# Products with constants on TensorE before each sampling round's sums, in a four-layer network on one core

## The chip, the cores and the metric

The kernel runs on one core of a Trainium2 chip. Its time is the device time of one execution in microseconds (us), given as the median of several runs. The engines are called as in the profile: PE multiplies matrices, DVE (VectorE) and ACT (ScalarE) do elementwise work, POOL (GpSimd) issues the indirect transfers here, and SP issues the other transfers.

## The reference, cut to what matters

Four images of 256 channels and 64x64 points pass through four layers. Each layer is `x = x + layer(groupnorm(x))`, all in float32. Layer 0 holds the sampling: for every point and each of four groups of 64 channels, nine places are computed from the data, and the image is read there with bilinear weights.

```python
def tap(xi, yi, w):
    valid = (xi >= 0) & (xi < Wi) & (yi >= 0) & (yi < Hi)
    idx = jnp.clip(yi, 0, Hi - 1) * Wi + jnp.clip(xi, 0, Wi - 1)
    v = jnp.take_along_axis(flat, idx.reshape(B, 1, -1), axis=2)
    return v.reshape(B, Cc, *xi.shape[1:]) * (w * valid.astype(img.dtype))[:, None]
...
dout = (samp * mr).sum(-1)                     # nine samples, weighted with a softmax
dout = jnp.einsum('nhwc,oc->nhwo', dout, outproj_w) + outproj_b
x2 = _bn(inp + dout, ...)
x3 = x2 * s                                    # squeeze and excite, s from the mean of x2
m = fc2(leaky_relu(fc1(x3)))
```

Before the sampling, layer 0 has a 1x1 convolution, a 3x3 depthwise convolution, and the 1x1 convolutions that give the places and the weights. Layer 1 is linear attention with a 5x5 depthwise convolution, layer 2 a 3x3 convolution with binarised weights, layer 3 an attention over a pooled image.

## The kernel before

**The sampling.** One image is sampled in 288 rounds (16 blocks of 18; `sample`, L558), four images in 1,152. A round of `gathered` (L592) has POOL issue four indirect transfers (L596), one for each group of channels: each reads, for 128 places, 1 KB from a table in HBM into a tile `g`. There are seven such tiles of four groups, so POOL can be seven rounds ahead of the sums. PE then multiplies what came with the weights `wm`, which ACT makes (L588), and so adds up the samples of each point: eight matmuls of 32 output rows and 128 columns (L603), into a quarter of a PSUM bank called `acc`. The tile has two halves of 256 columns; a half takes two rounds (`UR = 2`), and the halves take turns. After two rounds ACT copies the half to SBUF (`moved`, L608), PE turns it with two transposes (`turned`, L613), and ACT spreads the result (L623). These steps are put off by one, two and three rounds with a table `later`. At the end of a block, PE projects it (`project`, L636) and DVE and ACT finish it.

**What lies beside it.** `run` calls `beside`: after each sampling round it lets other generators go on, in proportion to their costs. Beside image 0 run the convolutions of images 1 to 3 (`convolve`: L373, L394) and their places (`offsets`, L496, with the 3x3 depthwise on DVE). Beside image 1 run the binarising of weights, then the two fully connected layers of image 0 (`feedforward`: L739, L749) and its layer 1 (L821, L870, L943, with the 5x5 depthwise on DVE, L178). Beside images 2 and 3 run the same for the image before, and layers 2 (L1085) and 3 (L1185, L1197, L1203) of the image before that. What is left then runs without sampling.

**The order.** In these stretches the instructions of PE, DVE, ACT and POOL stand on each engine in the order in which the program issues them (`manual_schedule`). SP's transfers are ordered by a scheduler. Each engine takes its instructions in turn, so on PE the sums of a round, the transposes and the matmuls of the other generators stand in one row.

The loop over the rounds, where the change is made:

```python
for i in range(NBLK * BR):
    b, r = divmod(i, BR)
    for f in later.pop(i, ()):
        f()
    if r % UR == 0:
        acc = next(accs)
    gathered(blocks[b], weights[0][0], acc, r)
```

`self.ident` is the 128x128 identity and `self.ow` the output projection's weights (128 partitions, four groups of 256 columns). Both are in SBUF from the start.

Of the kernel before, what the change touches and what calls it, by code (L numbers as in the profile page):

```python
# [17 lines left out]
P = 128  # L18
# [24 lines left out]
STEPS = 900  # L43
CONV, SECOND = NB * 22.5 + 11, 568
# [27 lines left out]
class Net:  # L72
    def __init__(self, ctx, tc, a, out):
        self.tc, self.nc, self.a, self.out, self.kept = tc, tc.nc, a, out, []
        e = ctx.enter_context
        self.cp = e(tc.tile_pool(name="const", bufs=1, side="left"))
        self.ps1 = e(tc.tile_pool(name="ps1", bufs=1, space=PSUM))
        self.mm = e(tc.tile_pool(name="mm", bufs=3, space=PSUM))
        self.banks, self.alone, self.spare = cycle(["mm"]), False, False
        self.dp = e(tc.tile_pool(name="scratch", bufs=1, space=DRAM))  # L80


# [29 lines left out]
    def groupnorm(self, pool, st, name):  # L112

        nc = self.nc
        mv = pool.tile([P, KT, 2], F32, name=name + "_mv")
        for k in range(KT):
            nc.vector.bn_aggr(mv[:, k, :], st[:, k].rearrange("p b s -> p (b s)"))
        yield 2
        pg = self.ps(name + "_pg")
        nc.tensor.matmul(pg[:, 0:KT], self.bd8, mv[:, :, 0], start=True, stop=True)  # L120
        mg = pool.tile([P, KT], F32, name=name + "_mg")
        nc.vector.tensor_copy(mg, pg[:, 0:KT])
        d = pool.tile([P, KT], F32, name=name + "_d")
        nc.vector.tensor_tensor(d, mv[:, :, 0], mg, ALU.subtract)
        nc.vector.tensor_tensor(d, d, d, ALU.mult)
        nc.vector.tensor_tensor(d, d, mv[:, :, 1], ALU.add)
        yield 2
        pv = self.ps(name + "_pv")
        nc.tensor.matmul(pv[:, 0:KT], self.bd8, d, start=True, stop=True)
        sc = self.rsqrt(pool, pv[:, 0:KT], EPS_GN, KT, name)  # L130
        bi = pool.tile([P, KT], F32, name=name + "_bi")
        nc.vector.scalar_tensor_tensor(bi, mg, -1.0, sc, ALU.mult, ALU.mult)
        yield 4
        return sc, bi

    def folded(self, pool, out, w, sc, bi, name):


        nc = self.nc
        n = w.shape[2] // P  # L140
        ps = self.ps(name + "_pb")
        for m in range(n):
            for k in range(KT):
                nc.tensor.matmul(ps[:, m:m + 1], w[:, k, m * P:(m + 1) * P], bi[:, k:k + 1], start=k == 0, stop=k == KT - 1)
        add = pool.tile([P, n], F32, name=name + "_add")
        nc.vector.tensor_copy(add, ps[:, 0:n])
        for k in range(KT):
            nc.scalar.activation(out[:, k], w[:, k], AF.Identity, scale=sc[:, k:k + 1])
        return add
# [104 lines left out]
    def binarise(self):  # L254
# [4 lines left out]
        with self.tc.tile_pool(name="bin", bufs=1, side="left") as sp, \  # L259
# [17 lines left out]
            for i in range(6):  # L277
                nc.tensor.matmul(ps[:, 0:C], self.ones, sums[:, i], start=i == 0, stop=i == 5)
# [27 lines left out]
    def weights(self, pool):  # L306
        nc = self.nc
        w = {}
        for key, name, n in (("cw", "conv_wT", C), ("iw", "inproj_wT", C), ("mw", "offmask_wT", 3 * Q)):
            w[key] = pool.tile([P, KT, n], F32, name=key)  # L310
            nc.sync.dma_start(w[key], self.a[name])

        ps = self.ps()
        for m in range(KT):
            dg = pool.tile([P, P], F32, name=f"dg{m}")
            nc.vector.tensor_scalar(dg, self.ident, self.inv[:, m:m + 1], None, ALU.mult)
            nc.tensor.matmul(ps[:, m * P:(m + 1) * P], self.ones, dg, start=True, stop=True)
        for k in range(KT):
            nc.vector.tensor_tensor(w["cw"][:, k], w["cw"][:, k], ps[:, 0:C], ALU.mult)
        return w  # L320

    def convolve(self, n, w, sp, bp, pads, used):
# [47 lines left out]
        def convolved(b, x, yb, m):  # L370
            ps = self.ps1.tile([P, 512], F32, name="cv", tag="vk")
            for k in range(KT):
                nc.tensor.matmul(ps, cw[:, k, m * P:(m + 1) * P], x[:, k], start=k == 0, stop=k == KT - 1)  # L373
            t = bp.tile([P, 512], F32, name="lk")
            after(1, lambda: nc.scalar.activation(t, ps, AF.Identity, bias=low[:, m:m + 1], scale=SLOPE))
            after(1, lambda: nc.vector.scalar_tensor_tensor(yb[:, m], ps, sh[:, m:m + 1], t, ALU.add, ALU.max))
            after(2, spread, b, yb, m)
# [9 lines left out]
        def projected(b, x, yb, xo, j2):  # L387

            ps = self.ps().rearrange("p (r o) -> p r o", o=C)
            for r in range(2):  # L390
                for h in range(2):
                    at = (4 * h + 2 * j2 + r) * W
                    for k in range(KT):
                        nc.tensor.matmul(ps[64 * h:64 * h + 64, r], yb[:, k, at:at + W], w["iw"][:, k], start=k == 0, stop=k == KT - 1)  # L394
            after(1, added, b, x, yb, xo, j2, ps)
# [80 lines left out]
    def offsets(self, n, c, y, mw, bp, used):  # L476
# [14 lines left out]
        for h in range(2):  # L491
            ps = self.ps().rearrange("p (j o) -> p j o", o=P)
            for j in range(4):
                at = (4 * h + j) * P
                for k in range(KT):
                    nc.tensor.matmul(ps[:, j, 0:3 * Q], t[:, k, at:at + P], mw[:, k], start=k == 0, stop=k == KT - 1)  # L496
            ob = self.row("offmask_b").unsqueeze(1).to_broadcast([P, 4, 3 * Q])
            nc.vector.tensor_tensor(off[:, 4 * h:4 * h + 4], ps[:, :, 0:2 * Q], ob[:, :, 0:2 * Q], ALU.add)
            nc.vector.tensor_tensor(ml[:, 4 * h:4 * h + 4], ps[:, :, 2 * Q:3 * Q], ob[:, :, 2 * Q:3 * Q], ALU.add)
            yield 3  # L500
# [57 lines left out]
    def sample(self, n, ssum):  # L558
# [33 lines left out]
        def gathered(sl, wm, acc, r):  # L592
# [8 lines left out]
            for x in range(2):  # L601
                for i in range(G):
                    nc.tensor.matmul(acc[32 * i:32 * i + 32, :], wm[:, r4, 4 * i + 2 * x:4 * i + 2 * x + 2, :],  # L603
# [29 lines left out]
        def project(b, m):  # L633
            po[m] = self.ps("po")
            for k in range(G):
                nc.tensor.matmul(po[m][:, 0:BR * OB], self.ow[:, k, m * P:(m + 1) * P], dT[b][:, k].rearrange("p r o -> p (r o)"), start=k == 0, stop=k == G - 1)  # L636
# [19 lines left out]
        for i in range(NBLK * BR):  # L656
# [3 lines left out]
            if r % UR == 0:  # L660
                acc = next(accs)
            gathered(blocks[b], weights[0][0], acc, r)
            if r == 0 and b + 1 < NBLK:
# [22 lines left out]
    def feedforward(self, n, ssum, st):  # L686
        nc, tc, a = self.nc, self.tc, self.a
        with tc.tile_pool(name=f"fa{n}", bufs=1, side="right") as sp, \
# [13 lines left out]
            for k in range(KT):  # L702
                nc.tensor.matmul(ps[0:64, 0:1], sd[:, k], mean[:, k:k + 1], start=k == 0, stop=k == KT - 1)
# [4 lines left out]
            for m in range(KT):  # L708
                ps = self.ps()
                nc.tensor.matmul(ps[:, 0:1], su[:, m * P:(m + 1) * P], dn, start=True, stop=True)  # L710
# [21 lines left out]
            for b in range(NB):  # L732
# [3 lines left out]
                for m in range(4 * KT):  # L736
                    ps = self.ps()
                    for k in range(KT):
                        nc.tensor.matmul(ps, f1[:, k, m * P:(m + 1) * P], x2[:, k], start=k == 0, stop=k == KT - 1)  # L739
# [6 lines left out]
                for m in range(KT):  # L746
                    ps = self.ps()
                    for k in range(4 * KT):
                        nc.tensor.matmul(ps, f2[:, k, m * P:(m + 1) * P], hm[:, k], start=k == 0, stop=k == 4 * KT - 1)  # L749
# [7 lines left out]
    def layer1(self, n, st, st2):  # L757
# [3 lines left out]
        with tc.tile_pool(name=f"la{n}", bufs=1, side="right") as sp, \  # L761
# [44 lines left out]
            def rows():  # L806


                for t, tiles in enumerate(((2, 4), (3, 5), (0, 1))):
                    new = lambda c: [self.padded(bp, 1, 20, 2, c, f"pad{i}", bufs=room(3) + (alone and i)) for i in range(2)]  # L810
                    pads = {0: new(0)}
                    for b in range(NB):
# [5 lines left out]
                        for i, m in enumerate(tiles):  # L818
                            ps = self.ps()
                            for k in range(KT):  # L820
                                nc.tensor.matmul(ps, qw[:, k, m * P:(m + 1) * P], x[:, k], start=k == 0, stop=k == KT - 1)  # L821
# [39 lines left out]
            def outer(t, kind, kv, vv, first, last):  # L861
# [15 lines left out]
                def added(i):  # L877
                    for j in range(2):
                        nc.tensor.matmul(sums[:, t, kind], kts[i][:, 1, j], kts[i][:, 0, j],
# [15 lines left out]
            def summed(t):  # L895
# [10 lines left out]
                for kind in range(2):  # L906
                    nc.tensor.matmul(pc[:, kind], ln[:, kind], pw[:, 2 * kind + t], start=True, stop=True)
                    nc.vector.tensor_copy(pw[:, 2 * kind + t], pc[:, kind])

            def output(c, qp, aq):  # L910
# [6 lines left out]
                def dens():  # L917
                    pd.append(self.ps("den"))
                    for h in range(2):
                        for j in range(4):  # L920
                            nc.tensor.matmul(pd[0][32 * j:32 * j + 32], ld[:, j, h], qh[h][j], start=h == 0, stop=h == 1)
# [6 lines left out]
                def head(h, j):  # L928
# [5 lines left out]
                    nc.tensor.matmul(pb[h, j], self.con("sel")[hs, i * P:(i + 1) * P], rd[0][hs], start=True, stop=True)  # L934
# [5 lines left out]
                def proj(h, m):  # L940
                    pr[h, m] = self.ps()
                    for j in range(4):
                        nc.tensor.matmul(pr[h, m], pw[:, j, m * P:(m + 1) * P], ot[h, j], start=j == 0, stop=j == 3)  # L943
# [83 lines left out]
    def layer2(self, n, st, st3, side="left"):  # L1027
# [3 lines left out]
        with tc.tile_pool(name=f"ca{n}", bufs=1, side=side) as sp, \  # L1031
# [45 lines left out]
            for b in range(NB):  # L1077
                v, xv = d, self.block(bp, self.x4_d[n], b, "x4")
                ahead = iter(())
                for m in range(KT):  # L1080
                    for half in range(2):
                        ps = self.long().rearrange("p (e q) -> p e q", e=2)
                        for i in range(12):
                            e, k, t = i // 6, i // 3 % 2, i % 3
                            nc.tensor.matmul(ps[:, e], w[:, k, t, 2 * half + e, m * P:(m + 1) * P], v[:, 2 * half + e, k, t:t + 8],  # L1085
# [14 lines left out]
    def layer3(self, n, st, wide=False):  # L1100
        nc, tc, a = self.nc, self.tc, self.a
        M = HW // 4
        with tc.tile_pool(name=f"na{n}", bufs=1, side="left") as sp, \
# [18 lines left out]
            for k in range(KT):  # L1122
                nc.vector.tensor_scalar(bb[:, k], self.ones, bi[:, k:k + 1], None, ALU.mult)
                nc.tensor.matmul(ps[:, 0:P], bb[:, k], gw[:, k], start=k == 0, stop=k == KT - 1)
# [13 lines left out]
            def first(b):  # L1138
                x = self.block(bp, self.x5_d[n], b, "x5", tag="pT")
                ps = self.ps()  # L1140
                for k in range(KT):
                    nc.tensor.matmul(ps, tw[:, k], x[:, k], start=k == 0, stop=k == KT - 1)
# [11 lines left out]
            def then(b, xq):  # L1154
                ps = self.ps()
                for k in range(KT):
                    nc.tensor.matmul(ps[:, 0:P], fw[:, k], xq[:, k], start=k == 0, stop=k == KT - 1)
                for k in range(KT):
                    nc.tensor.matmul(ps[:, P:2 * P], xq[:, k], gw[:, k], start=k == 0, stop=k == KT - 1)
# [13 lines left out]
            for b in range(NB):  # L1173
                m2 = bp.tile([P, 512], F32, name="m2")
                for j in range(4):
# [8 lines left out]
                    for i in range(2):  # L1184
                        nc.tensor.matmul(s[i], tv[:, 4 * b + j], ph[:, i * 512:(i + 1) * 512], start=True, stop=True)  # L1185
# [16 lines left out]
                    for m in range(8):  # L1202
                        nc.tensor.matmul(ps[:, 0:P + 1], pT[:, m], gt[:, m], start=m == 0, stop=m == 7)  # L1203
# [7 lines left out]
                for k in range(KT):  # L1211
                    ps = self.ps()
                    nc.tensor.matmul(ps, ww[:, k * P:(k + 1) * P], m2, start=True, stop=True)
# [170 lines left out]
```

## Time and profile before

| What | Value |
|---|---|
| median of 3 runs | 7,716.53 us (7,714.51 to 7,720.85) |
| the profiled execution | 8,695.07 us |
| its span | 8,693.3 us |
| instructions in it | 99,761 |
| mean granted clock of PE | 0.803 |
| busy: PE, weight loads, DVE, ACT, POOL | 5,880, 3,499, 4,818, 3,541, 4,935 us |
| gathers (L596) | 4,608 |
| matmuls of the sums (L603) | 18,432 in the trace |

The page gives each engine's busy time, the span in 40 slices (a digit is a tenth of the slice, and for PEclk a tenth of full clock), and groups of instructions. A row of a group has its line, engine, operation, `out<-in`, shapes and count, then busy time and mean nanoseconds of one, and then the idle time of the engine just before such instructions with what ended most of it ("<-"). "issue" is time in which the engine waited for nothing that the profile shows; "remote" is a release whose origin it does not show. The start of a matmul is measured and its end is modelled. The profiled execution is 979 us longer than the median, so times within it are set against its own span.

### The profile page before, as it was taken

Reading aid. Unit: us, or ns where it says so; the run is one execution under the profiler, and the core shown is the slowest. Engines: PE = TensorE matmul, PEld = TensorE weight load, DVE = VectorE, ACT = ScalarE, POOL = GpSimd, SP = SyncE. Lnnn points to the kernel's source line nnn. Section 1 sums busy time; section 2 is a strip of 40 time slices with the busy share of each in tenths; the row PEclk is TensorE's granted clock in tenths of the full one; section 3 lists DMA queues with packets and bytes.
Section 4 is the critical chain, followed back from the end, with each engine's and each line's share of the span. In section 5 each row is a group of like instructions: output and inputs, shape, how many; then the busy total and the mean of one; then the engine's idle time right before and its main releaser. Section 6 shows DMA issues by size and latency. Waiting matters only on the chain.

```text
span 8693.3 us, 99761 instructions
## 1 busy us (share of the span) xinstructions
PE 5880.0 (68%) x35776; PEld 3498.6 (40%) x35776; DVE 4817.7 (55%) x6045; ACT 3541.0 (41%) x10767; POOL 4934.7 (57%) x4870
## 2 busy tenths in 40 slices
PE   4454554448744446688876676888766778986899
PEld 2232222224323222234644443345544333664476
DVE  5344442443366667324776675228766762699833
ACT  2333333234444433334445443444454442456414
POOL 2666666466666666666666556666655560476410
PEclk7676766669866667799988887999878879998899
DMA  6454554444533334444543344445433342220131
GB/s 172 129 160 123 145 149 118 114 143 148 158 107 106 110 109 126 137 127 138 142 133 111 111 116 138 146 135 142 141 105 111 112 118 96 74 72 29 44 97 54
DMA packets 744383, 1031.75 MB, mean 119 GB/s; under 512 B 354128, under 2 KB 459984, under 8 KB 742352
## 3 DMA queue, kind: packets, MB, share of 16 engines
q0 software_dynamic: 221184, 604.27, 24.4%
q1 hardware_dynamic: 522704, 421.10, 16.4%
q8 instruction: 283, 4.64, 0.2%
q14 instruction: 212, 1.74, 0.1%
HBM read 856.39 MB, written 168.61 MB: 118 GB/s over the span
## 4 chain that ended last, share of the span: by engine, by line
PE 43%; another core or an unknown queue 17%; DVE 17%; ACT 13%; issue 8%; DMA 1%; POOL 0%; SPq 0%; ACTq 0%; DVEq 0%; POOLq 0%
DVE agg L178 10%; PE acc L603 6%; PE ps L739 5%; PE ps L749 5%; ACT wm L588 5%; PE ps L1085 4%; PE ps L821 3%; PE ps L943 2%; PE ps L1203 2%; PE s L1185 2%; PE po L636 2%; ACT dT L623 2%; ACT at L608 1%; PE rden L934 1%
## 5 line engine op out<-in xcount | busy, mean ns | idle before, releaser
L596 POOL DMA_INDIRECT g<-tab,sl x4608 | 4399.0, 955 | 2790.8 <-issue 1179.7
L178 DVE SCALAR_TENSOR_TENSOR agg<-pad,vec,agg 128x1024 f32<-128x1024 f32 x2280 | 2934.5, 1287 | 63.9
L603 PE MATMUL acc<-g,wm 128*32 128x128 f32 x18432 | 1012.4, 336 | 2022.6 <-ACT at L608 1471.8
L603 PEld LDWEIGHTS acc<-g,wm 128*32 128x32 f32 x18432 | 557.7, 129 | 2524.7 <-ACT at L608 1683.4
L588 ACT ACTIVATE wm<-sl,con 128x48 f32<-128x48 f32 x6144 | 1490.1, 366 | 26.0 <-remote 12.6
L1085 PE MATMUL ps<-xd,w 128*128 128x256 f32 x3072 | 741.0, 392 | 37.6 <-issue 30.1
L623 ACT COPY dT<-dp 64x128 f32<-64x128 f32 x1152 | 297.2, 258 | 985.8 <-remote 524.3
L1085 PEld LDWEIGHTS ps<-xd,w 128*128 128x128 f32 x3072 | 587.3, 196 | 159.0 <-issue 79.0
L739 PE MATMUL ps<-x2f,f 128*128 128x512 f32 x1024 | 502.3, 639 | 10.2 <-issue 5.1
L608 ACT COPY at<-acc 128x256 f32<-128x256 f32 x576 | 214.5, 372 | 712.8 <-remote 607.4
L821 PE MATMUL ps<-xr,qw 128*128 128x512 f32 x768 | 463.5, 733 | 21.8 <-issue 8.5
L724 DVE SCALAR_TENSOR_TENSOR hm<-ps,vec,lk 128x512 f32<-128x512 f32 x256 | 190.6, 750 | 502.4 <-ACT lk L741 375.2
L749 PE MATMUL ps<-hm,f 128*128 128x512 f32 x1024 | 463.6, 601 | 0.0
L741 ACT ACTIVATE lk<-ps,low 128x512 f32<-128x512 f32 x256 | 174.0, 687 | 514.7 <-PE ps L739 413.2
L636 PE MATMUL po<-dT,ow 128*128 128x288 f32 x1024 | 336.7, 477 | 56.5 <-issue 13.8
L875 ACT COPY kt<-pt 128x512 f32<-128x512 f32 x256 | 149.5, 585 | 544.8 <-remote 246.8
L1036 POOL TENSOR_TENSOR xd<-xp 128x640 f32<-128x640 f32 x64 | 79.8, 1275 | 497.3 <-DMA xq<-x 280.3
L1203 PE MATMUL ps<-gt,pT 128*128 128x129 f32 x2048 | 316.5, 315 | 47.1 <-ACT pT L1199 32.9
L613 PE MATMUL dp<-ident,at 128*128 128x128 f32 x1152 | 285.5, 336 | 77.1 <-ACT dT L623 53.4
L1203 PEld LDWEIGHTS ps<-gt,pT 128*128 128x128 f32 x2048 | 297.2, 226 | 98.8 <-ACT pT L1199 45.0
L1185 PE MATMUL s<-ph,th 128*128 128x512 f32 x512 | 289.2, 677 | 42.9 <-DVE ot L938 9.2
L739 PEld LDWEIGHTS ps<-x2f,f 128*128 128x128 f32 x1024 | 199.2, 203 | 253.3 <-issue 238.5
(243 smaller groups left out, 7710.6 us busy)
## 6 DMA issues: line engine op xcount, KB each, us to landing
g<-tab,sl POOLq DMA_INDIRECT x4608
x<-x SPq DMA_DIRECT2D x128, 512.0 KB
xr<-x SPq DMA_DIRECT2D x96, 512.0 KB
tab<-xo SPq DMA_DIRECT2D x192, 128.0 KB
x<-in_x SPq DMA_DIRECT2D x32, 512.0 KB
y<-yc SPq DMA_DIRECT2D x32, 512.0 KB
yb<-y SPq DMA_DIRECT2D x64, 256.0 KB
x<-yb SPq DMA_DIRECT2D x64, 256.0 KB
```

What stands on the lines that cost most here:

```text
L178: nc.vector.scalar_tensor_tensor(to, s, wt, acc, ALU.mult, ALU.add)
L588: nc.scalar.activation(wm[:, :, :, o], blocks[b][:, r:r + WR, G:], AF.Copy, scale=self.con("own")[:, o:o + 1])
L596: nc.gpsimd.indirect_dma_start(out=g[:, i, :], out_offset=None, in_=table, in_offset=bass.IndirectOffsetOnAxis(ap=sl.bitcast(I32)[:, r, i: ...
L603: nc.tensor.matmul(acc[32 * i:32 * i + 32, :], wm[:, r4, 4 * i + 2 * x:4 * i + 2 * x + 2, :], g[:, i, x * P:(x + 1) * P], start=x == 0, st ...
L623: nc.scalar.copy(dT[b][hs, :, r:r + UR], dp[u][hs, :, :, s, :].rearrange("p v g o -> p g v o"))
L636: nc.tensor.matmul(po[m][:, 0:BR * OB], self.ow[:, k, m * P:(m + 1) * P], dT[b][:, k].rearrange("p r o -> p (r o)"), start=k == 0, stop=k ...
L739: nc.tensor.matmul(ps, f1[:, k, m * P:(m + 1) * P], x2[:, k], start=k == 0, stop=k == KT - 1)
L749: nc.tensor.matmul(ps, f2[:, k, m * P:(m + 1) * P], hm[:, k], start=k == 0, stop=k == 4 * KT - 1)
L821: nc.tensor.matmul(ps, qw[:, k, m * P:(m + 1) * P], x[:, k], start=k == 0, stop=k == KT - 1)
L1085: nc.tensor.matmul(ps[:, e], w[:, k, t, 2 * half + e, m * P:(m + 1) * P], v[:, 2 * half + e, k, t:t + 8], start=i % 6 == 0, stop=i % 6 == 5)
L1185: nc.tensor.matmul(s[i], tv[:, 4 * b + j], ph[:, i * 512:(i + 1) * 512], start=True, stop=True)
L1203: nc.tensor.matmul(ps[:, 0:P + 1], pT[:, m], gt[:, m], start=m == 0, stop=m == 7)
```

## The change

A counter `work` adds up what each matmul in the program writes: twice the columns of its output, scaled by the output's partitions over 128. Transposes are not counted. Before the sums of a round, PE is given products of `ident` with columns of `ow` until the counter has reached 2,048; after the round's sums have been issued, the counter is set to zero. So a round's products depend on how much matmul work the other generators issued since the round before. The products are written to the part of `acc` that the coming sums overwrite: in an even round the whole half (256 columns, 512 of work each, at most four), in an odd round its second quarter (128 columns, 256 of work each, at most eight). Nobody reads them.

```diff
+ALIVE = 2048
...
-        self.banks, self.alone, self.spare = cycle(["mm"]), False, False
+        self.banks, self.alone, self.spare, self.work = cycle(["mm"]), False, False, 0
...
+    def of(self, out):
+
+        self.work += 2 * out.size() // P
+        return out
...
-                nc.tensor.matmul(ps, cw[:, k, m * P:(m + 1) * P], x[:, k], start=k == 0, stop=k == KT - 1)
+                nc.tensor.matmul(self.of(ps), cw[:, k, m * P:(m + 1) * P], x[:, k], start=k == 0, stop=k == KT - 1)
...
             if r % UR == 0:
                 acc = next(accs)
+            while self.work < ALIVE:
+                free = acc[:, r % UR * P:]
+                nc.tensor.matmul(self.of(free), self.ident, self.ow[:, 0, 0:free.shape[1]], start=True, stop=True)
             gathered(blocks[b], weights[0][0], acc, r)
+            self.work = 0
```

The wrapping with `self.of(...)` is the same at every other matmul of the program and changes none of them.

## The prediction

> **What bounds the kernel now.** I read the page's slices first, then the busy time by stage, the rows and waits of the gathers and their sums, and one stretch in order of time.
>
> ```profile
> POOL 2666666466666666666666556666655560476410
> PEclk7676766669866667799988887999878879998899
> L596 POOL DMA_INDIRECT g<-tab,sl x4608 | 4399.0, 955 | 2790.8 <-issue 1179.7
> L603 PE MATMUL acc<-g,wm 128*32 128x128 f32 x18432 | 1012.4, 336 | 2022.6 <-ACT at L608 1471.8
> ```
>
> Gathers fill the slices up to about 7,200 us, with POOL at 6 tenths whatever the other engines do. PE's clock is low in the first half. The sums (L603) issue for 1,012 us and stand idle for twice that, mostly until ACT's copy of the bank (L608).
>
> Busy time by sampling stage (images 0 to 3, then the rest without sampling); the columns are the stretch, its length, PE, weight loads, DVE, ACT and POOL with counts, clock, DMA share and GB/s:
>
> ```profile
> 137.00:1908.00 1771.00, 813.50 (x6476) 462.97 (x6476) 701.95 (x999) 597.50 (x2225) 1107.02 (x1152) 0.65 0.48 136
> 1908.00:3615.00 1707.00, 1018.38 (x6708) 533.92 (x6708) 979.22 (x1033) 681.63 (x2373) 1100.59 (x1153) 0.74 0.43 125
> 3615.00:5405.00 1790.00, 1332.42 (x8482) 795.13 (x8480) 1061.93 (x1281) 795.65 (x2575) 1096.56 (x1153) 0.86 0.45 129
> 5405.00:7210.00 1805.00, 1353.55 (x8583) 806.62 (x8585) 1064.50 (x1285) 798.10 (x2583) 1094.82 (x1152) 0.86 0.44 125
> 7210.00:8693.00 1483.00, 1282.86 (x5174) 859.88 (x5163) 914.03 (x1279) 638.24 (x958) 535.04 (x256) 0.92 0.21 66
> ```
>
> All four sampling stages take 1,707 to 1,805 us although PE's busy time differs by two thirds and its clock by a third. So neither sets the pace alone: what they share is 1,152 gathers. In order of time a gather starts every 1.255 us when nothing holds it (0.95 us and 0.30 us of issue), so 4,608 need 5,783 us. They take 7,054 us (137 to 7,191): POOL stands for 1,271 us, **18%**.
>
> What it stands for, in the waits of POOL:
>
> ```profile
> POOL g L596 <- issue: 1179.7, 3860, 0.6
> POOL g L596 <- PE acc L603: 648.2, 252, 36.7
> POOL g L596 <- remote: 578.1, 292, 3.5
> ```
>
> The first row is the 0.30 us between gathers. The others are waits for a buffer: there are 7, and PE's sums free them. "Remote" has no releaser in the records; it is 2 us at a time, at the start of a round. I take it for the same wait. And why PE is late, in order of time (image 1):
>
> ```profile
> 2996.21 0.37 ACT L608 COPY at<-acc 128x256 f32<-128x256 f32 x1
> 2996.63 1.08 PE L603 MATMUL acc<-g,wm 128*32 128x128 f32 x16 [1.41 <-ACT at L608]
> 2997.65 0.69 PE L613 MATMUL dp<-ident,at 128*128 128x128 f32 x2
> 2998.26 1.08 PE L603 MATMUL acc<-g,wm 128*32 128x128 f32 x16
> 3004.97 0.53 ACT L623 COPY dT<-dp 64x128 f32<-64x128 f32 x2 [5.54 <-remote]
> 3005.16 0.94 POOL L596 DMA_INDIRECT g<-tab,sl  x1 [1.94 <-remote]
> 3005.84 0.37 ACT L608 COPY at<-acc 128x256 f32<-128x256 f32 x1 [0.34 <-remote]
> 3006.27 1.08 PE L603 MATMUL acc<-g,wm 128*32 128x128 f32 x16 [6.93 <-ACT at L608]
> ```
>
> PE does two rounds, ACT copies them out, PE does the next two: a **loop PE, ACT, PE** of one turn in two rounds. In the built program the sums of every pair wait for the copy of the pair just before, although the two pairs use different halves of the bank. POOL is up to 7 rounds ahead, held by this loop.
>
> The profiled execution took 8,695.1 us (span 8,693.3 and 1.8 outside); the median without a profile is 7,716.5, 979 us less. The rest after 7,210 us is full of PE work, so I let nearly all of that fall on the sampling: 7,054 - 979 = 6,075 us, only 292 us above POOL's 5,783. In the timed runs POOL then stands for at most **5%**.
>
> **The Trainium skill.** "TensorE: Matmul & The Clock Gate", Part 1, says that PE runs at half clock until a window of some 3.4 us was busy, and returns to it after an idle one. The trace agrees on the window and is stricter on the rest: the clock changes in steps of 3.41 us; a slow window busy for 95% or more is followed by a full one in 9 of 10 cases, one busy for under 80% never; a full window busy for under 35% is never followed by another, so PE need not be idle to lose it. The sums take 1.08 us a round slow and 0.65 at full clock. I go by the trace: 1.75 us of products in a round of 5 don't keep the clock by themselves. "PSUM — Partial Sum Buffer", on bank collisions, has accesses of two engines to one bank and quadrant kept apart by semaphores, whichever columns they touch; the wait for ACT's copy of the other half, 1,472 us above, is such a one. The new products write to the same bank and so inherit it.
>
> **The change, part by part.** (1) *What is added.* In the built program 450 of 1,152 rounds get products: 176, 152, 61 and 61 of the four images; 209 of them are even rounds with 720 products of 256 columns, 241 odd ones with 1,612 of 128. Together 390,656 columns: 167,936, 128,000, 47,360 and 47,360. Each is issued to the chip in two passes, as every matmul but the transposes is (18,432 rows of L603 for 9,216 in the code). Price of a pass in a dense warm stretch:
>
> ```profile
> 8306.88 11.82 PE L1085 MATMUL ps<-xd,w 128*128 128x256 f32 x54
> ```
>
> 11.82 / 54 = 0.219 us for 256 columns with its weight load, 0.855 ns a column, so 1.71 ns a column of product: warm 287, 219, 81 and 81 us, twice that at half clock. A round without other work gets 1,024 columns, 1.75 us warm, 3.5 us cold.
>
> (2) *What clock that gives.* Busy time times clock is the work at full clock: now 529, 754, 1,146, 1,164 us, or 30%, 44%, 64%, 64% of the stages at clocks 0.65, 0.74, 0.86, 0.86. With the products it is 816, 973, 1,227, 1,245 us, or 46%, 57%, 69%, 69%; along those pairs the clock becomes about 0.75, 0.82, 0.88, 0.88 (an estimate from the rows above). The products then cost 383 + 267 + 92 + 92 = 834 us of PE's time. The work already there gets shorter: 813 (1 - 0.65/0.75) = 108, 1,018 (1 - 0.74/0.82) = 99, 1,332 (1 - 0.86/0.88) = 30, and 31: 268 us. Net PE is **566 us** longer busy: the saved time doesn't pay for the products.
>
> (3) *Where it stands.* In the built program an even round's first product carries the wait for ACT's copy, the products follow, then the sums. So they don't fill PE's idle time ahead of that wait; they start when it ends and push back the sums, the two transposes behind them, ACT's next copy, and every matmul of the other streams queued on PE. That is inside the loop. In odd rounds they stand between two things that were ready.
>
> (4) *What hides it.* POOL needs 5.02 us a round, and the products go to rounds with little other work: with 1.75 us of products, 0.65 of sums and 0.2 of a transpose, a warm round is half of that. Where PE isn't what POOL waits for, they cost nothing. I take as the share paid the share of time for which POOL stands: 5% (28 us) is the lower end, the profiled 18% (102 us) the upper; products in rounds that would have been used to catch up can bring 30% (170 us). I take **10%: 57 us**, as the loop gets longer where it had slack. 7,716.5 + 57 = 7,773. In a profiled execution I expect the 18%: about 8,797.
>
> (5) *What moves.* DVE and POOL keep their order. On ACT 12 scalings of weights (0.37 us each) stand behind some copies once. On SP some 65 of 1,559 transfers stand elsewhere, all among neighbours; the largest step is one block's index loads behind about 15 stores and table rows (0.3 to 0.7 us each to issue). They are wanted a block later, some 90 us, so I cost them at nothing; without that cover the longest wait of that line in SP's queue, 27.6 us, is the price. The count itself is made while building and costs nothing.
>
> **The rivals.** *Slower, fully paid.* If PE's loop and not POOL sets the pace in the timed runs too, most of the 566 us is paid: 60% is 340 us, 8,056. For it: POOL nearly always waits for PE in the profile. Against it: 979 us vanish without the profile.
> *Nothing.* If POOL's 1.255 us is the pace and products always lie beside it: 7,716. For it: equal stages at clocks of 0.65 to 0.86.
> *Faster.* The rounds that hold POOL are heavy ones, without products: they gain from a PE still warm from the round before (sums 1.08 to 0.65, transposes 0.69 to 0.44) and pay nothing. Images 0 and 1 have 591 of POOL's 1,271 us, so 136 of the 292; half of it back gives 7,648. In PE's total the point is a clock of 0.96 to 1.0 in images 0 and 1 (816/813, 973/1,018); it decides below that only if the light rounds are all hidden. For it: in image 0 POOL stands 0.32 us a gather while the clock is low and 0.22 while it is full. Against it: in image 1 that is 0.24 and 0.21, and in images 2 and 3, mostly at full clock, 0.30.
>
> **The numbers.** About 0.2%, 15 us, is what a measurement of this kernel tells from no change. Partly paid, 7,745 to 7,886, likeliest 7,773: 0.51. Fully paid, 8,056: 0.06. Nothing: 0.17. Faster, 7,648: 0.26. Range 7,640 to 7,900; left out are the fully paid case and the farther part of the faster one.
>
> **What would show it.** Right: sums' row unchanged in count, 4,664 new passes; clock near 0.75 in image 0; PE some 550 us busier before 7,210; even products released by ACT's copy; POOL's waits for PE longer. Wrong: POOL standing less than 1,271 us, or clocks above 0.9 in images 0 and 1 with the sums at 0.65 us throughout.

## The result and the profile after

The changed kernel takes 7,803.9 us (median of 4 runs, 7,799.6 to 7,809.0), the kernel before in the same comparison 7,716.8: a ratio of 1.0113 [1.0095, 1.013], **87 us more**.

One thing has to be known to read what follows. The kernel before takes 8,756 us on one of the three chips on which the experiments ran, and 7,721 and 7,723 on the other two (each chip was used for one set of runs). Its profile at the top of this document (8,695 us) lies near the one chip, and all its timed runs, and those of the changed kernel, agree with the other two; which chip that profile came from is not on record. So the profile after is set against another profile of the unchanged kernel, taken on one of the quick chips (the first experiment; span 7,723.4 us).

The page of the changed kernel: POOL and clock in 40 slices, then the gathers (L602, before L596), the sums (L609, before L603) and the products (L670).

```profile
POOL 2777777776777777767666567676666531966220
PEclk8999898899999988999898889999888899988899
L602 POOL DMA_INDIRECT g<-tab,sl x4608 | 4406.9, 956 | 1915.1 <-issue 1262.7
L609 PE MATMUL acc<-g,wm 128*32 128x128 f32 x18432 | 1005.0, 296 | 785.4 <-ACT at L614 455.7
L670 PE MATMUL acc<-ow,ident 128*128 128x128 f32 (+1 forms) x4664 | 923.1, 355 | 250.8 <-ACT at L614 250.6
```

The clock is 8 or 9 tenths from the first slice on. The sums take 1,005 us of PE; in the quick profile of the unchanged kernel they take 1,294. The products wait 250.6 us for ACT's copy (L614), a wait that was the sums'. PE is busy for 6,247.5 us against 5,933.0.

Busy time by stage in the unchanged kernel (quick chip; images 0 to 3, then the rest). The first number after the stretch is its length, the next PE's busy time; the last three are PE's clock, the DMA share and GB/s:

```profile
137.00:1603.00 1466.00, 961.34 (x6599) 500.87 (x6600) 715.37 (x1025) 606.68 (x2263) 1107.22 (x1153) 0.70 0.57 164
1603.00:3071.00 1468.00, 1097.99 (x6667) 550.05 (x6667) 967.19 (x1009) 674.18 (x2342) 1099.40 (x1152) 0.78 0.49 145
3071.00:4654.00 1583.00, 1253.25 (x8480) 760.69 (x8479) 1059.23 (x1281) 792.21 (x2575) 1097.65 (x1152) 0.89 0.50 146
4654.00:6238.00 1584.00, 1257.40 (x8489) 762.99 (x8482) 1059.96 (x1282) 792.27 (x2575) 1098.20 (x1152) 0.89 0.49 143
6238.00:7723.00 1485.00, 1284.01 (x5184) 861.55 (x5184) 913.02 (x1279) 637.95 (x958) 534.42 (x256) 0.92 0.21 66
```

And in the changed kernel:

```profile
138.00:1608.00 1470.00, 1078.78 (x8568) 719.40 (x8568) 715.14 (x1025) 606.85 (x2263) 1111.85 (x1152) 0.89 0.57 164
1608.00:3079.00 1471.00, 1154.79 (x8189) 692.17 (x8186) 967.49 (x1009) 675.03 (x2342) 1098.46 (x1153) 0.93 0.49 145
3079.00:4702.00 1623.00, 1324.31 (x9067) 841.10 (x9066) 1059.57 (x1281) 793.03 (x2575) 1098.18 (x1152) 0.91 0.49 142
4702.00:6324.00 1622.00, 1324.93 (x9073) 840.73 (x9072) 1060.40 (x1282) 793.04 (x2575) 1098.37 (x1152) 0.91 0.48 139
6324.00:7807.00 1483.00, 1283.88 (x5183) 860.98 (x5181) 912.85 (x1279) 638.18 (x958) 534.54 (x256) 0.92 0.21 66
```

Images 0 and 1 got 76% of the columns and are 4 and 3 us longer. Images 2 and 3 got 24% and are 40 and 38 us longer. The rest is unchanged. The clock rose in images 0 and 1 by 0.19 and 0.15, and that bought no time.

The waits of POOL, and of PE, show why (total us, times, longest; images 0 and 1, then images 2 and 3). In the unchanged kernel (quick chip):

```profile
POOL g L596 <- PE acc L603: 33.2, 32, 7.7
PE acc L603 <- DMA g<-tab,sl: 481.6, 606, 13.9
...
POOL g L596 <- PE acc L603: 316.5, 162, 6.6
PE acc L603 <- ACT at L608: 423.7, 178, 8.4
```

In the changed one:

```profile
POOL g L602 <- PE acc L609: 37.3, 38, 4.5
PE acc L609 <- DMA g<-tab,sl: 316.8, 392, 13.2
...
POOL g L602 <- PE acc L609: 397.2, 183, 6.6
PE acc L609 <- ACT at L614: 296.5, 129, 8.3
```

In images 0 and 1 PE waits for gathered data: it is early, and the products fill time in which it would have waited. Its waits for ACT's copy stay as they were there (321 us, then 311 with those of the products) and cost nothing. In images 2 and 3 PE waits for gathered data for 3 us in all in the unchanged kernel; POOL waits for PE, and for 81 us longer with the products.

One place, in the same rounds of image 2, shows the mechanism. Columns of a timeline: start, length, engine, instruction, and in brackets the idle time before and its releaser. Unchanged kernel (quick chip):

```profile
3883.38 0.20 ACT L631 COPY dT<-both 128x16 f32<-128x16 f32 x1 [5.46 <-DVE both L630]
...
3884.02 1.08 PE L603 MATMUL acc<-g,wm 128*32 128x128 f32 x16 [7.82 <-ACT at L608]
...
3894.97 0.37 ACT L608 COPY at<-acc 128x256 f32<-128x256 f32 x1
3895.39 1.06 PE L603 MATMUL acc<-g,wm 128*32 128x128 f32 x16 [3.50 <-ACT at L608]
3896.74 0.95 POOL L596 DMA_INDIRECT g<-tab,sl  x1 [0.44 <-PE acc L603]
...
4014.13 0.69 PE L613 MATMUL dp<-ident,at 128*128 128x128 f32 x2 [0.45 <-ACT dT L623]
4014.75 1.08 PE L603 MATMUL acc<-g,wm 128*32 128x128 f32 x16
4016.13 0.94 POOL L596 DMA_INDIRECT g<-tab,sl  x1 [0.94 <-PE acc L603]
```

Changed kernel:

```profile
3910.95 0.37 ACT L614 COPY at<-acc 128x256 f32<-128x256 f32 x1
3911.38 3.78 PE L670 MATMUL acc<-ow,ident 128*128 128x256 f32 x8 [3.50 <-ACT at L614]
3915.09 1.08 PE L609 MATMUL acc<-g,wm 128*32 128x128 f32 x16
3916.47 0.94 POOL L602 DMA_INDIRECT g<-tab,sl  x1 [4.19 <-PE acc L609]
...
4037.55 0.69 PE L619 MATMUL dp<-ident,at 128*128 128x128 f32 x2 [0.91 <-ACT dT L629]
4038.03 3.62 PE L670 MATMUL acc<-ow,ident 128*128 128x128 f32 x16
4041.58 1.08 PE L609 MATMUL acc<-g,wm 128*32 128x128 f32 x16
4042.97 0.94 POOL L602 DMA_INDIRECT g<-tab,sl  x1 [4.35 <-PE acc L609]
```

In the even round PE had waited 3.50 us for ACT in both kernels. After that wait the clock is low, so the products take 3.78 us for eight passes (0.47 each), not 1.75. The sums come 3.7 us later after the copy than before, and the gather that waits for their buffer stands 4.19 us in place of 0.44: POOL pays all of it. In the odd round it is the same, 4.35 for 0.94. These rounds are light on PE by the program's count, but POOL is at the end of its buffers there. Some 11 us before the even round, PE had stood 7.82 us for ACT's copy, which came behind an ACT instruction that had waited 5.46 us for DVE (L631, at the end of a block; in the changed kernel 7.95 and 5.58 us). So PE can be behind by waiting as well as by work, and a count of a round's work does not tell whether it has time to spare.

### The profile page after: what moved, and what is told of

The parts are those of the page before. It is cut to its first block, busy times and chain, and to the rows that moved or that the text cites. A ratio compares the mean times of both kernels' runs of the same rounds, so it can differ in the third digit from the quotient of the medians.

```text
span 7807.3 us, 108885 instructions
## 1 busy us (share of the span) xinstructions
PE 6247.5 (80%) x40440; PEld 3994.9 (51%) x40440; DVE 4811.5 (62%) x6045; ACT 3535.5 (45%) x10767; POOL 4942.1 (63%) x4870
## 4 chain that ended last, share of the span: by engine, by line
PE 40%; DVE 18%; POOL 7%; ACT 6%; issue 6%; DMA 3%; SPq 0%; DVEq 0%; POOLq 0%; ACTq 0%
DVE agg L184 12%; POOL g L602 6%; PE ps L749 6%; PE ps L759 6%; PE acc L609 4%; PE ps L1095 4%; PE acc L670 3%; PE ps L831 3%; PE ps L1213 2%; PE s L1195 2%; PE ps L953 2%; PE po L642 2%; DMA g<-tab,sl 1%; DVE mx L1196 1%; PE pt L1207 1%
## 5 line engine op out<-in xcount | busy, mean ns | idle before, releaser
L602 POOL DMA_INDIRECT g<-tab,sl x4608 | 4406.9, 956 | 1915.1 <-issue 1262.7
L609 PE MATMUL acc<-g,wm 128*32 128x128 f32 x18432 | 1005.0, 296 | 785.4 <-ACT at L614 455.7
L609 PEld LDWEIGHTS acc<-g,wm 128*32 128x32 f32 x18432 | 533.7, 114 | 1313.1 <-ACT at L614 592.3
L670 PE MATMUL acc<-ow,ident 128*128 128x128 f32 (+1 forms) x4664 | 923.1, 355 | 250.8 <-ACT at L614 250.6
L670 PEld LDWEIGHTS acc<-ow,ident 128*128 128x128 f32 x4664 | 759.9, 224 | 359.9 <-ACT at L614 312.6
L1095 PE MATMUL ps<-xd,w 128*128 128x256 f32 x3072 | 716.1, 385 | 6.0 <-DVE x L1079 3.5
L749 PE MATMUL ps<-x2f,f 128*128 128x512 f32 x1024 | 473.0, 609 | 1.8 <-ACT f L724 1.8
L614 ACT COPY at<-acc 128x256 f32<-128x256 f32 x576 | 214.5, 372 | 476.6 <-PE acc L609 442.8
L831 PE MATMUL ps<-xr,qw 128*128 128x512 f32 x768 | 403.9, 652 | 12.5 <-ACT pT L1209 5.6
L642 PE MATMUL po<-dT,ow 128*128 128x288 f32 x1024 | 294.4, 434 | 29.9 <-ACT dT L637 14.2
L1213 PEld LDWEIGHTS ps<-gt,pT 128*128 128x128 f32 x2048 | 274.9, 211 | 70.7 <-ACT pT L1209 31.9
L1213 PE MATMUL ps<-gt,pT 128*128 128x129 f32 x2048 | 290.9, 299 | 23.4 <-ACT pT L1209 19.5
L759 PEld LDWEIGHTS ps<-hm,f 128*128 128x128 f32 x1024 | 189.2, 190 | 225.9 <-issue 224.8
```

The source lines that it names most:

```text
L602: nc.gpsimd.indirect_dma_start(out=g[:, i, :], out_offset=None, in_=table, in_offset=bass.IndirectOffsetOnAxis(ap=sl.bitcast(I32)[:, r, i: ...
L609: nc.tensor.matmul(self.of(acc[32 * i:32 * i + 32, :]), wm[:, r4, 4 * i + 2 * x:4 * i + 2 * x + 2, :], g[:, i, x * P:(x + 1) * P], start=x ...
L642: nc.tensor.matmul(self.of(po[m][:, 0:BR * OB]), self.ow[:, k, m * P:(m + 1) * P], dT[b][:, k].rearrange("p r o -> p (r o)"), start=k == 0 ...
L670: nc.tensor.matmul(self.of(free), self.ident, self.ow[:, 0, 0:free.shape[1]], start=True, stop=True)
L749: nc.tensor.matmul(self.of(ps), f1[:, k, m * P:(m + 1) * P], x2[:, k], start=k == 0, stop=k == KT - 1)
L759: nc.tensor.matmul(self.of(ps), f2[:, k, m * P:(m + 1) * P], hm[:, k], start=k == 0, stop=k == 4 * KT - 1)
```

## The experiments

In what follows, **standing** is the sum over consecutive gathers of the time between their starts above 1.251 us, and **net PE** the increase of PE's busy time in a stage, products added less what the rest got shorter. Both are worked out from the traces.

**1. The unchanged kernel again.** No edit.

> The kernel before, unchanged, for a second profile. In the first one the waits of an origin that the records don't show took 17% of the chain, and the profiled execution was 979 us over the median; in the changed kernel's profile there are none, and it agrees with its median within 5 us. If the 979 us belong to the kernel before whenever it is profiled, this execution takes about 8,690 us again, with about 1,270 us of POOL standing. If they belonged to that one execution, it takes about 7,720 us, and POOL stands for some 290 us, nearly all of it in images 2 and 3.

Measured: 7,725.1 us with the profile on (span 7,723.4, clock 0.837), and no "remote" wait at all. So the 979 us between the first profile and the median do not come from the profiling as such. That they belong to a chip is read from experiments 5 to 8, where 13 runs of the kernel before take 8,734 to 8,774 us. As the prediction assumed, nearly all of the difference lies in the sampling: it lasts 6,099 us here and 7,054 there. Standing is 25, 29, 143 and 144 us in the four images.

**2. Products beside images 0 and 1 only** (295,936 of 390,656 columns).

```diff
-            while self.work < ALIVE:
+            while n < 2 and self.work < ALIVE:
```

> Products only beside images 0 and 1: 328 rounds, 295,936 of the 390,656 columns. In the changed kernel's profile POOL stands for 29 us in each of images 0 and 1 and 181 us in each of 2 and 3. Theory A (POOL's own pace hides the products beside images 0 and 1, and images 2 and 3 pay for theirs): within 0.2% of the kernel before, 7,700 to 7,732 us. Theory B (every product is paid at the same small share, as predicted): 76% of the columns, so 76% of 87 us, about 7,783 us. Theory C (a warmer PE helps there): below 7,700 us.

Measured: 7,723.6 us, ratio 1.0002 [0.9993, 1.001], at a clock of 0.903. Three quarters of the products, and whatever they move in the order of ACT and SP, neither cost nor gain anything.

**3. Products beside images 2 and 3 only** (94,720 columns).

```diff
-            while self.work < ALIVE:
+            while n > 1 and self.work < ALIVE:
```

> Products only beside images 2 and 3: 122 rounds, 94,720 columns. Theory A: the whole loss, about 7,804 us (87 us for 162 us of products at full clock). Theory B: 24% of it, about 7,738 us. A third theory, that the other order of SP's transfers costs the 87 us and not the products, has no fixed number for either kernel.

Measured: 7,801.3 us, ratio 1.0102 [1.0086, 1.0117], 79 us more. One quarter of the products is nearly the whole loss.

**4. Half of the set amount.**

```diff
-ALIVE = 2048
+ALIVE = 1024
```

> The bound is 1,024 instead of 2,048 in all images. Theory A: the loss goes with the columns that are left in images 2 and 3; with a bound of half, at most half the columns are left in each round that has any, so a loss of 20 to 45 us, 7,737 to 7,762 us. Theory B: half of the columns or less, 7,745 to 7,760 us. If it is the number of rounds with a product, or the added wait for ACT's copy, and not the time of the products: nearly the whole loss, about 7,790 us.

Measured: 7,750.4 us, ratio 1.0036 [1.0022, 1.0049], 28 us more. In images 2 and 3 there are 33,792 columns now, and 28 / 33,792 is 0.83 ns a column; in experiment 3 it is 79 / 94,720 = 0.83. That is half of the 1.71 ns that a column takes on PE.

**5 to 8, on the chip where the kernel before takes 8,756 us.** The first two exchange halves of the two PSUM tiles `acc` and `dp`, so that the sums of consecutive pairs of rounds go to two different tiles, and no longer wait for ACT's copy of the pair just before. First without products (5), then with (6):

```diff
-        def halves(name):
-
-            t = self.ps1.tile([P, 2, 256], F32, name=name, tag=name)
-            return cycle([t[:, 0], t[:, 1]])
-
-        accs, dps = halves("acc"), halves("dp")
+        banks = [self.ps1.tile([P, 2, 256], F32, name=name, tag=name) for name in ("acc", "dp")]
+        accs, dps = cycle([banks[0][:, 0], banks[1][:, 0]]), cycle([banks[1][:, 1], banks[0][:, 1]])
```

> The kernel before with the halves of two PSUM banks exchanged: bank one holds the sums of even pairs and the transposes of odd ones, bank two the others. The sums of a pair then no longer wait for ACT's copy of the pair just before; only the transposes wait for a copy, one round later. Theory A1 (the loop PE, ACT, PE of one turn in two rounds is what holds PE beside images 2 and 3, and so holds POOL): POOL stands clearly less than the 287 us of images 2 and 3, and the time falls by 40 to 150 us, to between 7,570 and 7,680 us. Theory A2 (PE's own work in heavy rounds holds it, the wait for the copy is slack): 7,700 to 7,735 us.

> The changed kernel with the banks exchanged in the same way: products as before, but none of them waits for ACT's copy of the pair just before. A1: the products fall into time in which PE stood, so the time is close to that of the exchanged kernel without products, within 30 us. A2: 80 us or more above it, as PE's time is what is paid.

Measured: 8,660.7 us without products, ratio to the kernel before 0.9888 [0.987, 0.9907], 96 us less, which by its size fits theory A1; 8,733.0 with them, 0.9968 [0.9954, 0.9982]. The products cost 72 us, which lies between the two readings of experiment 6 and nearer to A2. In the profile without products POOL stands 274 to 332 us in every image, with 749 us of its waits called "remote", and the products add 20 to 24 us of standing in each of the four images, the first two included. So what is hidden depends on the chip too. The changed kernel without the exchange was not run on this chip.

The next two leave the halves as they were. Experiment 7 has the products of experiment 3, but of 16 columns each; experiment 8 has the full ones up to twice the set amount (`n > 1` and `ALIVE = 4096`, 356,352 columns).

```diff
-            while self.work < ALIVE:
+            while n > 1 and self.work < ALIVE:
                 free = acc[:, r % UR * P:]
-                nc.tensor.matmul(self.of(free), self.ident, self.ow[:, 0, 0:free.shape[1]], start=True, stop=True)
+                nc.tensor.matmul(self.of(free)[:, 0:16], self.ident, self.ow[:, 0, 0:16], start=True, stop=True)
```

> Products only beside images 2 and 3, the same number (590), each written with 16 columns in place of 128 or 256, and counted as before. If the columns are the cost: 94,720 columns become 9,440, and the loss falls from 79 to about 10 us, 7,730 us. If the added instructions and waits are the cost, it stays near 7,800 us.

> Products only beside images 2 and 3, with a bound of 4,096 in place of 2,048: 328 rounds and 356,352 columns, 609 us of PE at full clock. With half the bound the loss was 28 us for 33,792 columns there, with the bound of 2,048 it was 79 us for 94,720: 0.83 ns a column both times, half of a column's 1.71 ns. Theory A: more rounds are now filled to 3.5 us of products, with sums, transposes and other work above POOL's 5.0 us, so the share paid rises from a half towards all: loss 350 to 600 us, 8,070 to 8,320 us. If the share stays at a half: about 8,020 us.

Measured: narrow 8,841.4, ratio 1.0095 [1.008, 1.0111], 85 us more; double 8,948.0, 1.0223 [1.0205, 1.0242], 192 us more. Experiment 7 fits its second reading: a tenth of the columns costs no less, so the price does not go with columns. Experiment 8 missed both of its readings (some 300 us, or 350 to 600): 3.8 times the columns brought the clock of the two images to 0.93. What the price goes with could not be read on this chip alone, for lack of the full products beside them. Hence the last four.

**9 to 12, on a chip where the kernel before takes 7,720.9 us:** the kernels of 5, 6, 7 and 3 once more.

> The kernel before with the halves of the two banks exchanged, so that the sums of a pair of rounds don't wait for ACT's copy of the pair just before. Theory (the loop of PE, ACT and PE holds POOL in images 2 and 3): on a chip where the kernel before takes about 7,720 us, POOL's standing of 143 and 144 us in images 2 and 3 falls by half or more, 7,580 to 7,690 us; on a chip where it takes about 8,756 us, again some 1.1% less. Rival (PE's own busy time or the gathers' transfers hold POOL there): within 15 us of the kernel before where that takes 7,720.

> The changed kernel with the same exchange of halves. Theory (products cost time because they lengthen the loop): on a chip where the kernel before takes 7,720 us, at most 30 us over the kernel of the exchange alone, against 87 us without it. Rival (the products cost PE's time in order, loop or not): 70 to 95 us over the exchange alone, as the 72 us seen where the kernel before takes 8,756.

Measured: without products **7,528.4 us, ratio 0.9749 [0.9735, 0.9762]**, 193 us less than the kernel before and the fastest version here; with products 7,565.7, 0.9798 [0.9784, 0.9811]. The products cost 37 us, where they cost 87 without the exchange. That is over the 30 that the theory gave, and far under the 70 to 95 of its rival.

Images 2 and 3 by busy time without products (the columns as above):

```profile
3062.00:4557.00 1495.00, 1244.95 (x8481) 751.92 (x8480) 1057.02 (x1281) 786.95 (x2575) 1101.28 (x1152) 0.90 0.52 154
4557.00:6056.00 1499.00, 1247.28 (x8483) 754.65 (x8482) 1057.75 (x1282) 787.46 (x2575) 1103.98 (x1152) 0.90 0.51 151
```

And the waits of POOL for the sums of the two tiles in the whole execution:

```profile
POOL g L592 <- PE acc L599: 64.3, 41, 8.3
POOL g L592 <- PE dp L599: 51.1, 50, 6.1
```

PE has as much to do as before, at 0.90 of its clock for 0.89, and yet the stages are 88 and 85 us shorter. POOL's waits for the sums fall from 349.6 us to 115.4, its standing in images 2 and 3 from 287 to 112. So in these two images it is mostly the loop of PE, ACT and PE that holds POOL, with whatever makes ACT's copy late, and not PE's work alone.

> Products in images 2 and 3 only, the same 590 in the same rounds, but each of 16 columns: 9,440 columns for 94,720. If the loss goes with the columns (PE's time): 5 to 20 us over the kernel before, of the 79 us that the full ones cost. If it goes with the number of products or with the wait for ACT's copy that the first one carries: 60 to 85 us, as the 85 us seen on the chip where the kernel before takes 8,756.

> The full products in images 2 and 3 only, beside the narrow ones on one chip. Where the kernel before takes 7,720 us: 79 us over it as seen before, so 7,795 to 7,810. Where it takes 8,756: if columns count, 60 us or more over the narrow ones, near 8,900; if the number of products or the wait counts, within 25 us of the narrow ones, near 8,850.

Measured: full 7,797.0, ratio 1.0098 [1.0083, 1.0114], 76 us more; narrow **7,865.7, 1.019 [1.0177, 1.0204], 145 us more**. Both readings of experiment 11 missed: a tenth of the columns costs nearly twice as much. Images 2 and 3 with the full products:

```profile
3072.00:4691.00 1619.00, 1326.48 (x9054) 841.44 (x9052) 1059.71 (x1281) 791.93 (x2574) 1096.68 (x1152) 0.91 0.48 143
4691.00:6313.00 1622.00, 1325.35 (x9074) 840.95 (x9078) 1060.38 (x1282) 792.83 (x2577) 1097.17 (x1152) 0.91 0.48 139
```

With the narrow ones, and one even round's products in order of time:

```profile
3067.00:4705.00 1638.00, 1345.97 (x8997) 868.03 (x8998) 1057.74 (x1279) 791.35 (x2570) 1097.73 (x1153) 0.88 0.48 141
4705.00:6354.00 1649.00, 1360.74 (x9071) 875.41 (x9072) 1059.25 (x1281) 793.67 (x2576) 1097.52 (x1152) 0.87 0.47 137
...
3905.73 1.78 PEld L670 LDWEIGHTS acc<-ow,ident 128*128 128x128 f32 x8 [3.74 <-ACT at L614]
3905.74 1.89 PE L670 MATMUL acc<-ow,ident 128*128 128x16 f32 x8 [3.50 <-ACT at L614]
```

Eight passes of 16 columns take 1.89 us at low clock, and the loads of 128 columns of weights beside them 1.78, so 0.22 each: as much as a pass of 128 columns in the odd round above (3.62 / 16 = 0.23), half of one of 256. The load sets the price of a narrow pass. The Trainium skill ("TensorE: Matmul & The Clock Gate", "LDWEIGHTS (loading the stationary operand)") has the load's time go with the columns of the weights and not with their rows. The changed kernel's trace agrees on the rows: the shortest load of 64 rows by 128 columns takes 0.182 us, of 128 by 128 0.186, of 128 by 32 0.106, though a quarter of the columns is not a quarter of the time. So the narrow products still take 101 us of PE an image, the full ones 125. And they leave the clock at 0.88 and 0.87, under the 0.89 without products, where the full ones bring 0.91: the rest of PE's work gets 51 and 57 us shorter with the full products (1,253 - (1,326 - 125), and so on) but only 8 in image 2, and none in image 3, with the narrow ones. Why narrow passes do less for the clock was not tried by itself.

Standing and net PE of images 2 and 3 together, each against its own reference (1 for the upper four rows, though 11 and 12 ran on the other quick chip; 9 for the last). The share is the added standing by the net PE time:

| Kernel | net PE, us | more standing, us | share | loss in images 0 and 1: net PE, standing |
|---|---|---|---|---|
| changed kernel | 139 | 78 | 0.56 | 174, 7 |
| half (4) | 63 | 32 | 0.51 | 80, 1 |
| full, images 2 and 3 (12) | 141 | 74 | 0.52 | none added |
| narrow (11) | 196 | 120 | 0.61 | none added |
| exchange with products (10) | 114 | 33 | 0.29 | 170, -5 |

One rule covers the rows without the exchange: in images 2 and 3, 0.5 to 0.6 of the net PE time is paid, in images 0 and 1 next to nothing. With the exchange it is 0.29. Set against the first profile, which is not of the same set of runs, experiment 7 gives 197 and 116 us (0.59) and experiment 8 456 and 210 us (0.46). Of the 133 us by which the narrow kernel's profiled execution is longer, some 16 lie behind the sampling; I did not follow them.

## Why the prediction was right, and where it was not

The direction, the mechanism and roughly the size held: "partly paid", 7,773 us forecast for 7,804 measured. But two terms of the sum were off in opposite ways: the net PE time was 1.8 times too large, the share paid 2.8 times too small. That their product came out near is luck. Of the signs named, the passes, the release by ACT's copy and POOL's longer waits for PE came; a clock near 0.75 and a PE some 550 us busier did not. POOL standing less than 1,271 us, named as a sign of being wrong, came too (425 us), but that sum belonged to the first profile: against the quick one it rose from 341.

**(1) What is added.** Right: 4,664 passes in the trace. They take 923 us of PE against 834 forecast.

**(2) The clock.** Mis-sized. Along the rows of the first profile the forecast was 0.75, 0.82, 0.88 and 0.88; measured are 0.89, 0.93, 0.91 and 0.91. So much more of PE's time is saved: 610 us (923 - 313), the sums alone 289, against 268 forecast. Net PE is 313 us longer busy (117, 57, 71 and 68 by image), not 566. In experiment 6 products did bring 0.79, 0.84, 0.88 and 0.88, near the forecast (0.66, 0.73, 0.86 and 0.87 without, in experiment 5): the rows were read rightly, but the timed runs are not like them. The clocks alone do not give the 610 us. With the clocks of the two quick profiles, the forecast's own formula gives 205 + 177 + 28 + 28 = 438 us, an estimate. Its premise, that busy time times clock is the work, does not hold: image 0 without products is 529 us by it in the first profile and 961 * 0.70 = 673 in the quick one (its sums 299 and 497 us busy). With the products these sums fell to 336 us, to 0.68, where the clocks' ratio is 0.79. That fits sums which are issued piece by piece as their data comes, and less so with products ahead of them: PE stood for gathered data 606 times in images 0 and 1, and 392 times then. The clock rule also left a gap between 35% and 80%. In the changed kernel's trace, of the full windows busy for 50 to 65% only 14% (of 204) are followed by a slow one, of those busy for 35 to 50% it is 84% (of 90); a warm round with products, 1.75 + 0.65 + 0.2 of 5.02 us, is busy for some 52%.

**(3) Where it stands.** Right, and seen in the timeline: the even products took over the wait for ACT's copy and pushed back the sums. The loop carries more than half of the price on a quick chip: 87 us became 37 once the sums no longer waited for the copy just before. In the odd round shown the products did the same harm without a wait of their own.

**(4) What hides it.** This is the step that failed: one share, 10%, for all products. Measured over all it is 87 / 313 = 28%, but the mean says little: it is 0.04 in images 0 and 1 (7 of 174 us) and 0.56 in images 2 and 3. POOL's standing in the timed runs was judged well, 292 us forecast for 341 in the quick profile, 5.6% of the sampling. What was missed is that 287 of them lie in images 2 and 3. The first profile spread it nearly evenly (331, 266, 349, 346 us); in images 0 and 1 it has 357 us of POOL's waits called "remote", which the quick chips' profiles don't have. The prediction did name the reason for a high share, "products in rounds that would have been used to catch up", and gave it 30%; it is what the place in image 2 shows. The profiled execution, forecast at 8,797, took 7,809: that sum was made against the first profile.

**(5) What moves.** Right as far as tried: experiment 2 contains the moves that go with its products and costs nothing. Those of images 2 and 3 were not tried without their products. But experiments 11 and 12 issue the same products in the same places and cost 145 and 76 us, so the order alone does not set the price.

**The rivals.** Fully paid (8,056) fell: even beside images 2 and 3 a bit over half is paid. Nothing (7,716) holds for images 0 and 1. Faster (7,648) fell for lack of anything to gain: clocks of 0.89 and 0.93 came, though not the 0.96 to 1.0 of its break-even, but POOL stands only 25 and 29 us there. Even a wrong sign of the net PE time would have changed little in those two images.

## What to carry to other kernels

Filling an engine's idle time to keep its clock up buys nothing where another engine sets the pace; ask stage by stage who waits for whom, and count as free only the stretches in which the engine waits for its data. Work that is put into "light" rounds costs time if these are the rounds in which a late engine catches up. If a profiled execution is 13% longer than the timed runs, find out why before taking shares of waits from it; and look for the wait that closes the loop first: here, exchanging two half tiles was worth 193 us on one chip and 96 on another, and the products were worth none.

## What the runs showed of the hardware that was not expected

- The same unchanged kernel took 7,721 and 7,723 us on two chips and 8,756 on a third. The longer time is in the sampling: in the same kernel POOL stands 1,255 us in experiment 5 and 154 in experiment 9. Much of it is in waits that the trace calls "remote" (749 us of POOL's in experiment 5, none in 9). The profile does not show what releases them, and the cause stays open.
- A product of 16 columns held PE as long as one of 128 (0.22 us a pass at low clock) and did less for the clock: 0.88 and 0.87 with narrow products, 0.91 with full ones, 0.89 with none.
- The clock of images 0 and 1 rose from 0.70 and 0.78 to 0.89 and 0.93 with products in 176 and 152 of their 288 rounds.
